# Layer 2's attention on one Trainium2 core: head scaling on GpSimd, other evictions, other waits

## The chip, the cores and the metric

The kernel runs on one core of one Trainium2 chip. The metric is the time of one launch on the device, in microseconds (us). Five runs of the kernel before gave 2965.73, 2966.24, 2966.6, 2967.86 and 2974.98; the median is 2966.6. A further execution was profiled and left the trace that is read here.

The engines are TensorE (PE in the profile; its weight loads are PEld), VectorE (DVE), ScalarE (ACT), GpSimd (POOL) and SyncE (SP, which issues most DMAs). SBUF is the on-chip memory with 128 partitions, PSUM the accumulators that TensorE writes. Each engine runs its own instructions in order and waits on semaphores for the others.

## The reference

The network has four layers of the form half feed-forward, attention, half feed-forward, on a residual of 2 batches x 1024 tokens x 128 features in f32. Layer 2 is the one that is changed:

```python
x = x + 0.5 * _L2_ffn_ref(_layernorm(x), ...)    # eight experts, top 2
x = x + _L2_attn_ref(_layernorm(x), ...)
x = x + 0.5 * _L2_ffn_ref(_layernorm(x), ...)
```

The attention has 16 heads of 64. Queries and keys are normalised per head, scores are clamped by a tanh, and the softmax runs over all 1024 keys:

```python
x = _rmsnorm(tokens, norm_w)
q, k, v = split(x @ Wq), split(k), split(v)        # k, v from x @ Wkv
q, k = _head_rmsnorm(q, q_gamma), _head_rmsnorm(k, k_gamma)
sim = jnp.tanh(einsum('bhid,bhjd->bhij', q, k) / 50) * 50 * 64 ** -0.5
out = einsum('bhij,bhjd->bhid', softmax(sim), v)
return out.reshape(b, n, 1024) @ Wo
```

with `_head_rmsnorm(x, gamma) = x / max(norm(x), 1e-12) * (gamma + 1) * 8`. The feed-forward sends each token to its two best of eight experts (128 to 512 and back, gelu), adds the input, normalises per expert and mixes the two results by their gates.

## The kernel before

The residual `x` stays in SBUF as [128, 16, 128]: 16 tiles of 128 tokens, in four chunks q = 0 to 3 of 512. Chunks 0 and 1 are batch 0, chunks 2 and 3 batch 1.

**Order.** TensorE's order is the order in which the Python code issues matmuls; the other engines' orders are chosen by the framework's scheduler from dependencies and modelled times. Side work is put into TensorE's order by threads: `c.later(key, pieces)` queues a list of functions and numbers, `c.tick(us)` advances a modelled clock, and a number in the list holds the thread back by so many modelled us before its next function. `c.need(key)` runs what is left of a thread at once. These numbers place work; they are not measured times.

**The mixture pass of layer 2** works on two halves of two chunks each: (0,1) and (2,3) before the attention, (0,2) and (1,3) after it. `l2_ffn_prep` (line 1227) normalises a chunk (`norm_pieces`, line 183: statistics on VectorE, apply as xn partly on ScalarE at line 164, transposes on TensorE at line 172) and stores it to DRAM as `xd`. After routing, `L2Experts` (line 1346) works on groups of up to four tiles of gathered tokens. `gather` (lines 1373 to 1382) reads a group's rows from `xd` into a buffer `xg` with one indirect DMA per tile, issued by GpSimd. `fetch` (line 1395) loads the experts' weights through SP. `ahead` (line 1404) decides how many groups are gathered in advance. A group is transposed (line 1428), multiplied (hidden at lines 1440 and 1449, output at 1456), combined on VectorE (lines 1474 to 1487; the last reader of `xg` is line 1474), and stored to DRAM as `yd` (line 1488). `l2_back` (line 1510) returns a half: sixteen indirect DMAs on GpSimd read rows of `yd` into `yg` (line 1525), and two `add` steps (lines 1532 to 1542, VectorE), one for each chunk, form the inverse standard deviation and add to `x`. After each, `l2_attn_prep` normalises that chunk for the attention.

**The attention** (`L2Attention`, line 1557) runs eight groups: batch b and f = 0 to 3, four heads each. `project(b, f)` makes two lists of eight pieces, one per tile j of 128 tokens:

- `product(j)`: matmuls for v (line 1583) and for q and k together (line 1587), into two of the shared PSUM banks; VectorE copies them to `v` (line 1584) and `raw` (line 1594); GpSimd squares `raw` into `sq` (line 1596); VectorE sums it per head into `hsq` (line 1597). After the eighth, `inv_sqrt` (lines 115 to 120, a bit trick and three Newton steps on VectorE) makes `hrq`, the inverse norms of all eight tiles.
- `turn(j)`: VectorE scales `raw` in place by `hrq` (line 1605), TensorE transposes it (`ppt`, line 1609), and VectorE writes it with the gains to `tr` (line 1612).

`run` works a group through in 16 slots. A slot computes scores for two key tiles (line 1673, four matmuls of 512 columns), ScalarE applies tanh (line 1680, twice) and exp (line 1681), and `mix` of the slot before adds up the probabilities and multiplies them by v (`po`, line 1706). The sums for the first half of the keys are made on GpSimd (`acp`: lines 1693, 1695, 1696), those for the second half on VectorE (`acc`: lines 1698 to 1702). After four slots `divide` sums `acc` over partitions (line 1718), copies to `rn` on ScalarE (line 1720), inverts it (line 1721) and scales `po` into `aoT` (line 1722), the last two on VectorE. The products of the next group are in slots 0 to 7, its turns in slots 10 to 14. The output projection of the group before stands in slots 8 and 9 (`py`, line 1650) and is added to `x` by VectorE (line 1659). Three `pe` buffers hold probabilities; two pairs of PSUM banks hold scores.

The first group has nothing to hide behind: `first` (line 1621) issues its products between the last experts and its turns after them, and the attention's first scores wait for all eight turns. The second half's return, called with `step` 1 in `l2_back`, runs during groups 0 and 1; the norms for the second mixture pass run in group 4 (chunks of batch 0), at the end of group 7 and behind it.

Of the kernel before, what the change touches and what calls it, by code (L numbers as in the profile page):

```python
# [11 lines left out]
F32 = mybir.dt.float32  # L12
# [3 lines left out]
ALU = mybir.AluOpType  # L16
# [3 lines left out]
P = 128  # L20
NT = 16
TB = 8
# [1201 lines left out]
    return h  # L1224


def l2_ffn_prep(c, w, keep, h, a):
    nc = c.nc
    q, r = h["qs"][a], {}
    tiles = slice(4 * a, 4 * a + 4)  # L1230
    norm = norm_pieces(c, r, q, by=8)

    def begin():
        if "o" not in h:
            h["o"] = keep.tile([P, 2, TB, 8], F32, tag="ho", name="ho", bufs=2)
            h["g"] = keep.tile([P, 2, TB], F32, tag="hg", name="hg", bufs=2)

    def store():
        nc.sync.dma_start(out=h["xd"][512 * a : 512 * a + 512, :].rearrange("(j p) d -> p j d", p=P), in_=r["xn"])

    def chosen():
        h["ready"] += 1
        if h["ready"] == 2:
            c.later(("route", h["name"]), l2_route(c, w, keep, h) + h["then"])

    gates = gate_pieces(
        c, r, q, w["router"], 8, w["beta"],
        places=lambda: ([h["o"][:, k, tiles, :] for k in range(2)], [h["g"][:, k, tiles] for k in range(2)]),
    )
    return [begin] + norm[:3] + [store] + norm[3:] + gates[:1] + [chosen] + gates[1:]  # L1250
# [95 lines left out]
class L2Experts:  # L1346
# [28 lines left out]
    def gather(self):  # L1375

        n = self.gathered
        h, g = self.groups[n]
        self.xg[n] = self.keep.tile([P, 4, P], F32, tag="xg", name="xg", bufs=4)
        for j, i in enumerate(g):  # L1380
            at = bass.IndirectOffsetOnAxis(ap=h["tok"][:, i : i + 1], axis=0)
            self.nc.gpsimd.indirect_dma_start(self.xg[n][:, j, :], None, h["xd"], at)
        self.gathered += 1
# [20 lines left out]
    def ahead(self, k):  # L1404

        h = self.groups[self.tiles[k][0]][0]
        if "tok" not in h:
            for a in range(2):
                self.c.need(("half", h["qs"][a]))
            self.c.need(("route", h["name"]))  # L1410

        some = 2 if any(self.c.waits(("back", h["name"])) for h in self.halves) else 3
        while self.gathered < min(self.tiles[k][0] + some, len(self.groups)) and self.routed(self.gathered):
            self.gather()
        while self.fetched < min(k + 6, len(self.tiles)) and self.routed(self.tiles[self.fetched][0]):
            self.fetch()
# [93 lines left out]
def l2_back(c, keep, h, parts, step):  # L1510


    nc = c.nc
    pieces = [[], []]
    for p, (a, j, done) in enumerate(parts):
        tiles = [(u, v) for u in range(2)[a] for v in range(4)[j]]
        b = {}

        def fetch(k, lo, tiles=tiles, b=b):
            if k + lo == 0:  # L1520
                b["yg"] = keep.tile([P, 2, 4, P + 1], F32, tag="yg", name="yg", bufs=2)
            for n in range(lo, lo + step):
                u, v = tiles[n]
                at = bass.IndirectOffsetOnAxis(ap=h["si"][:, TB * k + 4 * u + v :][:, 0:1], axis=0)
                nc.gpsimd.indirect_dma_start(b["yg"][:, k, n, :], None, h["yd"], at)

        def add(a=a, j=j, tiles=tiles, b=b, done=done):
            sc = keep.tile([P, 2, 4], F32, tag="bsc", name="bsc", bufs=2)
            var = keep.tile([P, 2, 4], F32, tag="bvar", name="bvar", bufs=2)
            yg = b["yg"]  # L1530

            c.tc.keep_in_program_order(nc.vector.tensor_copy(var, yg[:, :, :, P]))
            flat = lambda t: t.rearrange("p k n -> p (k n)")
            inv_sqrt(c, flat(sc), flat(var), 1.0 / P, 1e-6)
            g = h["g"].rearrange("p k (u v) -> p k u v", u=2)[:, :, a, j]
            nc.vector.tensor_tensor(
                sc.rearrange("p k (u v) -> p k u v", u=g.shape[2]), sc.rearrange("p k (u v) -> p k u v", u=g.shape[2]), g, ALU.mult
            )
            for n, (u, v) in enumerate(tiles):
                x = c.x[:, 4 * h["qs"][u] + v, :]  # L1540
                for k in range(2):
                    nc.vector.scalar_tensor_tensor(x, yg[:, k, n, 0:P], sc[:, k, n : n + 1], x, ALU.mult, ALU.add)
            done()

        gathers = [x for k in range(2) for lo in range(0, 4, step) for x in (partial(fetch, k, lo), 1.05 * step)]
        pieces[p] = gathers, add
    (one, add_one), (two, add_two) = pieces
    if step == 1:
        return [8.0] + one + two + [add_one, 14.0, add_two, 0.1]
    return [5.0] + one + two[:1] + [3.0, add_one, 1.2] + two[2:] + [8.0, add_two, 0.1]  # L1550


def l2_attn_prep(c, w, rs, q):

    e = float(np.finfo(np.float32).eps)
    return norm_pieces(c, rs[q], q, 1.0 + e, 1e-5 * e, w["norm"])


class L2Attention:
# [6 lines left out]
    def project(self, b, f):  # L1566


        c, nc, w, rs = self.c, self.c.nc, self.w, self.rs
        side, bank = self.side, c.bank  # L1570
        mine = self.pool if f % 2 else side
        raw = side.tile([P, TB, 2, 4, 64], F32, tag="raw", name="raw")
        tr = mine.tile([P, 2, 2, S], F32, tag="tr", name="tr", bufs=1)
        v = mine.tile([P, TB, 4, 64], F32, tag="v", name="v", bufs=1)
        ssq = side.tile([P, TB, 2, 4], F32, tag="hsq", name="hsq", bufs=2)
        rq = side.tile([P, TB, 2, 4], F32, tag="hrq", name="hrq", bufs=2)

        def product(j):
            c.need((self.key, 2 * b + j // 4))
            lhsT = rs[2 * b + j // 4]["xT"][:, j % 4 * P : (j % 4 + 1) * P]  # L1580
            pv = bank("pv")[:, 0:256]
            off = 1024 + f * 256
            nc.tensor.matmul(pv, lhsT=lhsT, rhs=w["wkv"][:, off : off + 256], start=True, stop=True)
            nc.vector.tensor_copy(v[:, j].rearrange("p h d -> p (h d)"), pv)
            pp = bank("pqk").rearrange("p (n h d) -> p n h d", n=2, h=4)
            for n, wt in enumerate((w["wq"], w["wkv"])):
                nc.tensor.matmul(
                    pp[:, n].rearrange("p h d -> p (h d)"),
                    lhsT=lhsT,
                    rhs=wt[:, f * 256 : (f + 1) * 256],  # L1590
                    start=True,
                    stop=True,
                )
            nc.vector.tensor_copy(raw[:, j], pp)  # L1594
            sq = side.tile([P, 2, 4, 64], F32, tag="sq", name="sq", bufs=1)
            nc.gpsimd.tensor_mul(sq, raw[:, j], raw[:, j])  # L1596
            nc.vector.tensor_reduce(ssq[:, j], sq, AX.X, ALU.add)
            if j == TB - 1:

                nc.vector.tensor_scalar(ssq, ssq, 1e-24, None, ALU.max)  # L1600
                inv_sqrt(c, rq, ssq, 1.0, 0.0)

        def turn(j):
            rj = raw[:, j]
            nc.vector.tensor_tensor(rj, rj, rq[:, j].unsqueeze(3).to_broadcast([P, 2, 4, 64]), ALU.mult)
            pt = bank("ppt").rearrange("p (n k t) -> p n k t", n=2, k=2)
            for n in range(2):
                for k in range(2):
                    nc.tensor.transpose(
                        pt[:, n, k, :], rj[:, n, 2 * k : 2 * k + 2, :].rearrange("p h d -> p (h d)"), c.ident  # L1610
                    )
            nc.vector.tensor_tensor(
                tr[:, :, :, j * P : (j + 1) * P],
                pt,
                w["gm"][:, :, 2 * f : 2 * f + 2].unsqueeze(3).to_broadcast([P, 2, 2, P]),
                ALU.mult,
            )

        return (tr, v), [partial(product, j) for j in range(TB)], [partial(turn, j) for j in range(TB)]
# [407 lines left out]
def macaron(ctx: ExitStack, tc: tile.TileContext, dram: dict, out: bass.AP):  # L2027
    nc = tc.nc
    c = Ctx(tc, dram)
# [34 lines left out]
    with ExitStack() as s1:  # L2064
        with tc.tile_pool(name="w0", bufs=1) as p0:
            w = l0_weights(c, p0)
            sets = l2_sets(c, dpool)
            r = [chunks() for _ in range(8)]
# [19 lines left out]
        w2 = l2_consts(c, keep2)  # L2088
        s2 = ctx.enter_context(ExitStack())
        wa = l2_attn_weights(c, s2.enter_context(c.pool("w2a")))  # L2090
        def halves(n, parts):

            hs = [l2_half(c, dpool, f"{n}{k}", qs) for k, qs in enumerate(parts)]

            def prep(q):
                h = next(h for h in hs if q in h["qs"])
                c.later(("half", q), l2_ffn_prep(c, w2, keep2, h, h["qs"].index(q)))

            return hs, prep

# [148 lines left out]
```

## Time and profile before

| | us |
|---|---|
| median of five runs | 2966.6 |
| profiled execution | 2975.98 |
| its span, first to last instruction | 2974.2 |
| first mixture pass of layer 2, experts | about 1616 to 1764 |
| attention, from its first scores | 1795.4 to about 2545 |
| second mixture pass | about 2550 to 2690 |

| group of the attention | 0 | 1 | 2 | 3 | 4 | 5 | 6 | 7 |
|---|---|---|---|---|---|---|---|---|
| first scores at, us | 1795.4 | 1883.2 | 1988.6 | 2076.6 | 2164.7 | 2272.8 | 2360.8 | 2448.8 |
| until the next group (7: its scores), us | 87.8 | 105.4 | 88.0 | 88.0 | 108.1 | 88.0 | 88.0 | 74.6 |

The granted clock of TensorE over the whole span is 0.94 of full speed. A line of the profile's groups names the line in the code, the engine, the operation, output and inputs, and how often it ran; then busy time and mean duration in ns, and the idle time ahead of it with what ended it. In the tables of stretches, each engine's busy us is followed by its number of instructions, then the granted clock, the share of DMA time and GB/s. In a timeline, start and duration stand first.

### The profile page before, as it was taken

The numbers are of one execution on the slowest core, as the hardware profiler recorded it, in microseconds if no ns is written. First come the engines' busy times: TensorE is split into PE (matmuls) and PEld (weight loads), VectorE is DVE, ScalarE is ACT, GpSimd is POOL, SyncE is SP. The second block draws the span as 40 slices with busy tenths as digits, with TensorE's granted clock in tenths as the row PEclk, the third lists the DMA queues.
The fourth block names the chain that finished last, engine by engine and source line by source line (L and its number), as shares of the span: only waits on it lengthen the run. The fifth ranks groups of instructions, "written<-read, shape, count | busy, mean of one in ns | idle before, by whom it ended". The sixth has DMA issues, their size and how long they took to land. (4 is left out here: it accounts for less than half of the span.)

```text
span 2974.2 us, 42437 instructions
## 1 busy us (share of the span) xinstructions
PE 2648.7 (89%) x14226; PEld 1511.3 (51%) x14226; DVE 2081.1 (70%) x6492; ACT 1605.3 (54%) x3188; POOL 953.1 (32%) x909
## 2 busy tenths in 40 slices
PE   7899999999989888888887959899998999879999
PEld 5544444444465455444445843334433433777667
DVE  4567667766646878868766567777777775668874
ACT  3355555555533355666632526667666778444553
POOL 0022122112102544445443445334543443342110
PEclk9899999999989868999997989999999999889999
DMA  5000000000000000000012730000000001660000
GB/s 124 8 15 15 15 8 15 15 15 8 8 22 1 1 1 1 1 1 2 18 40 73 207 84 9 1 1 1 1 1 8 1 28 39 164 176 22 1 5 11
DMA packets 69768, 86.52 MB, mean 29 GB/s; under 512 B 14334, under 2 KB 49935, under 8 KB 68912
## 3 DMA queue, kind: packets, MB, share of 16 engines
q1 hardware_dynamic: 56620, 70.14, 8.3%
q0 software_dynamic: 4992, 10.27, 1.7%
q10 hardware_dynamic: 7940, 3.41, 0.4%
q8 instruction: 114, 1.87, 0.2%
q14 instruction: 102, 0.84, 0.1%
HBM read 66.18 MB, written 12.38 MB: 26 GB/s over the span
## 5 line engine op out<-in xcount | busy, mean ns | idle before, releaser
L1680 ACT ACTIVATE pe<-ps 128x1024 f32<-128x1024 f32 x256 | 249.5, 1023 | 208.5 <-PE ps L1673 208.2
L507 ACT ACTIVATE pe<-ps,nm 128x512 f32<-128x512 f32 (+3 forms) x384 | 220.0, 579 | 113.8 <-DVE nm L505 111.9
L1673 PE MATMUL ps<-tr 64*128 64x512 f32 x1024 | 264.9, 637 | 0.0
L1706 PE MATMUL po<-pe,v 128*64 128x512 f32 x1024 | 250.8, 611 | 0.9 <-ACT pe L1681 0.9
L1681 ACT ACTIVATE pe<-pe 128x2048 f32<-128x2048 f32 x128 | 244.8, 1912 | 4.0
L341 DVE SCALAR_TENSOR_TENSOR x<-py,gates,x 128x128 f32<-128x128 f32 x448 | 134.0, 345 | 147.2 <-PE py L311 147.0
L494 PE MATMUL ps<-kT,qT 64*128 64x512 f32 (+3 forms) x768 | 181.7, 552 | 39.2 <-ACT pe L507 28.1
L505 DVE TENSOR_REDUCE nm<-ps 128x2 f32<-128x256 f32 (+1 forms) x192 | 182.9, 952 | 45.6 <-PE ps L494 42.8
L522 PEld LDWEIGHTS ptp<-ident,pe 128*128 128x128 f32 x1152 | 126.8, 143 | 113.8 <-issue 82.4
L522 PE MATMUL ptp<-ident,pe 128*128 128x128 f32 x1152 | 174.2, 287 | 4.7 <-ACT pT L104 2.2
L104 ACT COPY pT<-ptp 128x512 f32<-128x512 f32 x192 | 92.1, 480 | 159.8 <-PE ptp L522 158.4
L457 POOL TENSOR_TENSOR kT<-tab 128x512 f32<-128x512 f32 x32 | 54.4, 1699 | 367.1 <-DVE tab L456 367.0
L536 PE MATMUL po<-pT,v 128*64 128x512 f32 (+3 forms) x768 | 168.6, 518 | 0.0
L1449 ACT ACTIVATE hT<-ph,w1b 128x128 f32<-128x128 f32 x368 | 105.6, 369 | 100.7 <-issue 61.0
L1706 PEld LDWEIGHTS po<-pe,v 128*64 128x64 f32 x1024 | 62.8, 137 | 174.5 <-issue 159.7
L1693 POOL TENSOR_TENSOR acp<-pe 128x1024 f32<-128x1024 f32 x32 | 78.3, 2446 | 220.5 <-ACT pe L1681 197.3
L1673 PEld LDWEIGHTS ps<-tr 64*128 64x128 f32 x1024 | 91.2, 192 | 104.7 <-issue 73.0
L1058 POOL TENSOR_SCALAR pe<-pe,rs 128x256 f32<-128x256 f32 (+7 forms) x128 | 95.2, 756 | 138.7 <-DVE rs L1055 55.9
L311 PEld LDWEIGHTS py<-l3f_w,hT 128*128 128x128 f32 x1024 | 125.6, 196 | 24.5 <-issue 20.3
L1596 POOL TENSOR_TENSOR sq<-raw 128x512 f32<-128x512 f32 x64 | 88.7, 1385 | 141.2 <-DVE raw L1594 107.0
L1440 PE MATMUL ph<-xgT,w1b 128*128 128x128 f32 x736 | 111.0, 299 | 22.6 <-ACT hT L1449 12.6
L494 PEld LDWEIGHTS ps<-kT,qT 64*128 64x128 f32 x768 | 60.7, 192 | 136.9 <-ACT pe L507 62.9
(418 smaller groups left out, 6340.4 us busy)
## 6 DMA issues: line engine op xcount, KB each, us to landing
w1b<-sets SPq DMA_DIRECT2D x92, 258.0 KB, 5.0
b2g<-sets SPq DMA_DIRECT2D x92, 128.0 KB, 4.3
two<-two SPq DMA_DIRECT2D x64, 128.0 KB, 2.3
yd<-y SPq DMA_DIRECT2D x20, 258.0 KB, 4.7
l2f_w<-in_l2f_w SPq DMA_DIRECT2D x2, 2048.0 KB
sets<-in_l2f_w SPq DMA_DIRECT2D x1, 2048.0 KB
xd<-xn SPq DMA_DIRECT2D x8, 256.0 KB, 3.6
l3f_w<-in_l3f_w SPq DMA_DIRECT2D x2, 1024.0 KB
```

Of the source, the lines that this page charges most:

```text
L311: nc.tensor.matmul(py[:, j, :], lhsT=hT[:, k, j * P : (j + 1) * P], rhs=w2[:, e, k, :], start=(k == 0), stop=(k == hc - 1),)
L341: c.nc.vector.scalar_tensor_tensor(x, py[:, j, :], rs[q]["g"][:, j, e : e + 1], x, ALU.mult, ALU.add)
L494: nc.tensor.matmul(ps[:, h, :W], lhsT=u["qT"][r, q0 : q0 + P], rhs=u["kT"][r, gk * 512 : gk * 512 + W], start=True, stop=True,)
L505: nc.vector.tensor_reduce(nm, ps[:, :, :W], AX.X, ALU.max, negate=True)
L507: nc.scalar.activation(u["pe", n][:, h, i, :W], ps[:, h, :W], AF.Exp, bias=nm[:, h : h + 1], accum_out=u["rs"][:, n, i, h : h + 1],)
L522: nc.tensor.transpose(pt[:, i * P : (i + 1) * P], u["pe", n][:, h, i, j * P : (j + 1) * P], c.ident)
L536: nc.tensor.matmul(u["po", n][r, lo * P :], lhsT=u["v"][:, BLOCKS[n][1] * 4 + j, cols], rhs=u["pT", n, j][h][:, lo * P :], start=(j == 0), ...
L1440: nc.tensor.matmul(ph[:, a * P : (a + 1) * P], lhsT=t[:, a * P : (a + 1) * P], rhs=xT[n][:, j * P : (j + 1) * P], start=True, stop=True,)
L1673: nc.tensor.matmul(ps[:, h, :], lhsT=tr[r, 1, p, k * P : (k + 1) * P], rhs=tr[r, 0, p, q * 512 : (q + 1) * 512], start=True, stop=True,)
L1680: nc.scalar.activation(pe[:, j], ps, AF.Tanh, scale=1.0 / 50.0)
L1681: nc.scalar.activation(pe, pe, AF.Exp, scale=50.0 * 0.125)
L1706: nc.tensor.matmul(u["po"][r, :], lhsT=u["v"][:, k, 2 * u["p"] + h, :], rhs=pe[:, j, h, :], start=(k == 0), stop=(k == TB - 1),)
```

## The change

Five edits, all in layer 2:

1. Head scaling: `raw` times `hrq` moves out of `turn`'s own place into `scale(j)`. Turn 0 issues the scales of tiles 0, 1 and 2, turn j that of tile j + 2. It runs on GpSimd, except in the first group, where even tiles stay on VectorE. There are 64 such instructions in all, eight in a group.
2. In the first group, the PSUM copies to `v` and `raw` run on ScalarE instead of VectorE.
3. `xg` has six buffers instead of four, and groups are gathered up to five ahead instead of two or three.
4. The return of the second half (`step` 1) waits 40 modelled us instead of 8.
5. The waits ahead of a norm's apply and of its transposes become (10, 9) instead of (4.5, 4) for two kinds of chunk: chunks 2 and 3 in the attention's norm, and chunks 0 and 1 in the second mixture pass. All other chunks of these two functions keep (4.5, 4).

```diff
-def l2_ffn_prep(c, w, keep, h, a):
+def l2_ffn_prep(c, w, keep, h, a, late):
...
-    norm = norm_pieces(c, r, q, by=8)
+    norm = norm_pieces(c, r, q, by=8, wait=(4.5, 4.0) if late else (10.0, 9.0))
...
-        self.xg[n] = self.keep.tile([P, 4, P], F32, tag="xg", name="xg", bufs=4)
+        self.xg[n] = self.keep.tile([P, 4, P], F32, tag="xg", name="xg", bufs=6)
...
-        some = 2 if any(self.c.waits(("back", h["name"])) for h in self.halves) else 3
-        while self.gathered < min(self.tiles[k][0] + some, len(self.groups)) and self.routed(self.gathered):
+        while self.gathered < min(self.tiles[k][0] + 5, len(self.groups)) and self.routed(self.gathered):
             self.gather()
...
     if step == 1:
-        return [8.0] + one + two + [add_one, 14.0, add_two, 0.1]
+        return [40.0] + one + two + [add_one, 14.0, add_two, 0.1]
...
-    return norm_pieces(c, rs[q], q, 1.0 + e, 1e-5 * e, w["norm"])
+    return norm_pieces(c, rs[q], q, 1.0 + e, 1e-5 * e, w["norm"], wait=(4.5, 4.0) if q < 2 else (10.0, 9.0))
...
-        mine = self.pool if f % 2 else side
+        mine, first = self.pool if f % 2 else side, b == f == 0
...
-            nc.vector.tensor_copy(v[:, j].rearrange("p h d -> p (h d)"), pv)
+            copy = nc.scalar.copy if first else nc.vector.tensor_copy
+            copy(v[:, j].rearrange("p h d -> p (h d)"), pv)
...
-            nc.vector.tensor_copy(raw[:, j], pp)
+            copy(raw[:, j], pp)
...
+        def scale(j):
+            rj = raw[:, j]
+            e = nc.vector if first and j % 2 == 0 else nc.gpsimd
+            e.tensor_tensor(rj, rj, rq[:, j].unsqueeze(3).to_broadcast([P, 2, 4, 64]), ALU.mult)
+
         def turn(j):
+
+            for k in (0, 1, 2) if j == 0 else (j + 2,):
+                if k < TB:
+                    scale(k)
             rj = raw[:, j]
-            nc.vector.tensor_tensor(rj, rj, rq[:, j].unsqueeze(3).to_broadcast([P, 2, 4, 64]), ALU.mult)
...
-                c.later(("half", q), l2_ffn_prep(c, w2, keep2, h, h["qs"].index(q)))
+                c.later(("half", q), l2_ffn_prep(c, w2, keep2, h, h["qs"].index(q), n == 1 or q >= 2))
```

In the changed kernel's numbering the lines of this part stand 1 or 2 lower up to the projection (gathered rows are transposed at 1426, `v` is copied at 1583, `raw` at 1593) and 7 higher after it: scale 1605, `ppt` 1616, `tr` 1619, output projection 1657, its add to `x` 1666, scores 1680, tanh 1687, exp 1688, `acp` 1700 to 1703.

The engines' orders follow from the scheduler. Of the built program: TensorE's order differs from before only in the places of the transposes at line 172 for chunks 2 and 3 (group 1, slots 12 and 15 instead of 5 and 8) and of the norm and router steps in groups 4 and 5, two slots later. On GpSimd, all gathers of `xg` stand ahead of the sixteen of `yg` in the first mixture pass; at its end come seven squares, two gathers of `yg`, a square, seven gathers, four scales, seven gathers. In each later group the order is the eighth square, scale 0, the acp of slot 8's first key tiles, scales 1 to 7, and that sum's two further acp. On SP, the loads of layer 3's weights wait for the attention's last `aoT`, since the allocator places them elsewhere; before, they ran in its last group.

## The prediction

> **What bounds the kernel now.** I read the page's shares first, then TensorE's waits by line, then busy time stretch by stretch, then the order of work on the engines that feed TensorE.
>
> ```profile
> PE 2648.7 (89%) x14226; PEld 1511.3 (51%) x14226; DVE 2081.1 (70%) x6492; ACT 1605.3 (54%) x3188; POOL 953.1 (32%) x909
> ```
>
> TensorE bounds nearly everything, so only its gaps and its clock can give time. In layer 2 the waits (line, releaser: total us, times, longest) and the stretches (length, busy per engine, granted clock) are:
>
> ```profile
> PE pt L172 <- ACT xn L164: 17.1, 4, 8.2
> PE ppt L1609 <- DVE raw L1605: 13.2, 4, 10.3
> PE pt L1428 <- DMA xg<-xd,r_tok: 11.6, 4, 5.0
> PE py L1650 <- DVE x L1659: 5.1, 5, 1.0
> PE ppt L1609 <- DVE x L1659: 4.8, 4, 1.2
> PE pt L1428 <- DVE v L1584: 4.7, 1, 4.7
> ...
> 1700.00:1750.00 50.00, 33.90 (x234) 29.89 (x232) 29.10 (x137) 16.89 (x55) 24.71 (x25) 0.86 0.55 142
> 1750.00:1800.00 50.00, 32.72 (x155) 24.21 (x156) 33.79 (x113) 7.83 (x21) 21.10 (x21) 0.73 0.14 39
> 1883.00:1989.00 106.00, 92.76 (x396) 38.46 (x396) 79.78 (x168) 67.53 (x59) 38.15 (x20) 0.94 0.00 1
> 1989.00:2077.00 88.00, 85.01 (x386) 35.34 (x384) 67.20 (x78) 63.44 (x53) 40.86 (x20) 1.00 0.00 1
> ```
>
> The first two stretches are the end of the first mixture pass and the first head group's projection: TensorE is idle a third of the time, at a clock of 0.86 and 0.73. Groups 2, 3, 5 and 6 (such as 1989:2077) take 88.0 us with 85.0 busy. Groups 1 and 4 take 105.4 and 108.1: residual adds, norms and routing of token chunks run in them, and line 172 waits for ScalarE's xn.
>
> What matters for a move from VectorE to GpSimd is how they meet:
>
> ```profile
> 2039.01 2.25 DVE L119 SCALAR_TENSOR_TENSOR nw<-nh,nw 128x64 f32<-128x64 f32 x1
> 2044.93 7.68 DVE L1605 TENSOR_TENSOR raw<-raw,hrq 128x512 f32<-128x512 f32 x6
> ...
> 2038.77 2.41 POOL L1693 TENSOR_TENSOR acp<-pe 128x1024 f32<-128x1024 f32 x1 [1.47 <-ACT pe L1681]
> 2044.54 2.35 POOL L1695 TENSOR_TENSOR acp<-acp,pe 128x1024 f32<-128x1024 f32 x1 [3.36 <-ACT pe L1681]
> 2046.97 2.69 POOL L1696 TENSOR_TENSOR acp<-acp,pe 128x1024 f32<-128x1024 f32 x1
> ...
> L719 POOL TENSOR_TENSOR eq<-eq,fi 128x512 f32<-128x512 f32 x32 | 33.8, 1056 | 34.0 <-DVE fi L718 20.3 <-DVE ln_rs L120 9.7 <-DVE md L129 3.0
> ```
>
> A 0.23 us VectorE operation took 2.25 because GpSimd's acp ran; six scales of 0.68 took 7.68 instead of 4.1 beside two acp; the second acp grew from 2.35 to 2.69. Instructions with two SBUF operands wait for the other engine's whole instruction, and they alternate. Copies from PSUM, reductions and reciprocals were not slowed.
>
> **The change, part by part.** All figures are against the profiled execution: 2975.98 us, span 2974.2, so 1.8 outside it, which is left alone. It is 9.4 above the median of 2966.6; savings are subtracted from the median.
>
> *End of the first mixture pass (six xg buffers, eager gathers).* Sixteen yg gathers (1699.0 to 1719.3, 1.25 us each) stand on GpSimd ahead of the last seven xg gathers. TensorE then waits 4.96, 1.91 and 2.99 us (1717.9 to 1729.2) and 1.07 for xn. In the changed order all xg gathers precede the yg ones; the last waits only for the buffer released before 1689.5. The three waits go, but line 172 needs the norm whose scale VectorE finishes at 1722.67; 0.88 for two xn on ScalarE gives 1723.6. It started at 1730.8: gain 7.
>
> *First group's evictions on ScalarE.* VectorE's queue delays the 4.66 us wait at 1746.8 (on v's copy, behind a residual add and norm) and waits of 1.03, 0.41 and 1.35 among the last products. ScalarE is idle for most of 1736 to 1770 and a 128x512 copy from PSUM costs it 0.57 to 0.59: the 4.66 falls to about 0.6, gain 4. Its cover is that idle ScalarE; without it, eight tiles x (0.58 + 0.4) = 8 us. Four products are left after the experts. They began at 1764.8, and the last square ended at 1781.2, as copies, squares and five yg gathers followed one another; at 1.75 us a product on TensorE (0.43 each for its matmul pairs, plus a copy), they take 1764.8 + 7 + 0.6 + 1 + 1 = 1774.4 (the last copy, its square, and what two gathers hold that up): gain 6.7. Together the last square ends 17.7 earlier, near 1763.5.
>
> *The scales of that group.* Even tiles stay on VectorE, odd ones go to GpSimd, where seven of the second half's yg gathers stand ahead: 7 x 1.25 = 8.8, to 1772.3. That the 40 us wait sends this return into the attention is not what the issue order shows. Four scales at 1.04 to 1.3 end at 1777 and the last turn, with its tr, at 1779. Attention began at 1795.4: 16.4, less 1.4 because TensorE still idles before the turns and starts them, as now (1778.7 to 1799.2), at half clock: **15 gained**. Ends: 8 (only the gathers and copies, scales at 1.70 as line 457 has on average) and 18 (no gathers ahead).
>
> *Group 0* has 6.5 us more than a steady group in its slots 8 to 13, where the first half-return's add lies. It moves to group 1: **4.5**, between 0 and 6.5.
>
> *Steady groups.* Each has a 1.02 and a 1.20 wait for x (line 1659), queued behind the eight scales. These go: 2.2. GpSimd gets eight operations of about 1.05 (line 719: same shape, same broadcast factor), in a burst of seven before the two acp of k2=1. These end up to 1.1 later, and tr(1) of slot 11 waits behind the acc that needs them: 0.5 given back. 1.7 x 4 = **6.8**; between 4 x 2.2 = 8.8 and, with scales of 1.7 to 1.9, 4 x -2 = -8.
>
> *Group 1.* Both adds and both norms now come after hrq, at about 2041 in the coordinates of the group shown. There GpSimd has scale, acp, seven scales, two acp: 8 x 1.05 + 3 x 2.35 = 15.5. VectorE's chain (nine steps of inverse root, eight adds, statistics, nine steps again, ln_off) is some 30 tiny instructions with two SBUF operands, 0.16 to 0.27 each; its first ten each wait for one whole GpSimd instruction. Its end, 2052 without that (2041 plus 5 for the add, as at 1931.3 to 1936.2, and 6 for the norm), becomes about 2066; two xn of 0.88 stand on ScalarE between the tanh of slot 10, and that slot's second tanh, due at 2049, runs at 2068, with the exp and the next scores behind it: TensorE stops about 18 us. The second norm costs 5, half clock after both 3.5 each (as after the gaps of 1919 and 1944, for 7 us each): 85.8 + 18 + 5 + 7 = 115.8 against 105.4: **10.4 lost**. Ends: a stop of 5 and 4 at the clock (95.4, 10 gained), and 14 lost (scales at 1.5: 8 x 0.45).
>
> *Group 4.* The xn of the next pass's norm moves ahead of the exp of slot 9. ScalarE waits there about 12.8 us, of which TensorE has 9 of stop, then 4 for the second norm, 4 at half clock, 6 of transposes and routing: 85.8 + 23 = 108.8 against 108.1: **0.9 lost** (−8 to +9, by the same arithmetic).
>
> *The second mixture pass.* A shift in the allocator's addresses makes layer 3's weights (two loads of 1 MB and fourteen small ones) wait for the last aoT instead of hiding in the last group. They stand on SP's queue ahead of the eighth tile set and the last xd store (issued 2553 and 2554), delaying both by 4 to 6 us; the first is needed near 2567, so **1 lost**, between 0 and 8.
>
> Sum: 15 + 4.5 + 6.8 − 10.4 − 0.9 − 1 = 14.0.
>
> The Trainium skill, "Perfetto Trace Analysis", Optimizing Scalar/DVE Operations, warns that these two engines share an SBUF read port, so that moving work between them might not help; taken literally, the steady groups' term would be 0 and the sum 7. The rows favour a part of the gain, since what goes are two waits, not work. "GPSIMD Engine Reference", Engine selection, puts two-input elementwise work at about twice VectorE's time; as an estimate from the row of 0.68 that is 1.36 per scale, 0.3 over line 719, and the sum would be 14.0 − 7 x 0.3 x 2 = 9.8.
>
> **The rivals.**
> *A, little collision.* If VectorE's tiny steps slip between GpSimd's instructions, group 1 gains 10, group 4 breaks even and the steady groups get their 8.8: 15 + 4.5 + 8.8 + 10 − 1 = 37, so 2929. For it: the six scales lost 3.6 us to two acp of 5.0 together, less than one for one. Against it: the 0.23 us step that cost 2.25.
> *B, slower.* The chain in group 1 against GpSimd's burst, with ScalarE blocked at xn behind it. Price: group 1 −14, group 4 −8 by the same stop, steady groups −8 as each scale is stretched; gains shrink to 8 + 2; second pass −1: −21, so 2988. It decides from the point where the chain ends over 30 us after hrq (the forecast has 25).
> *C, nothing.* The first pass's gain halves, because the odd scales wait for all 14 yg gathers left (17.5 us instead of 8.8), and steady groups gain 0.5 each: 6 + 4.5 + 2 − 10.4 − 0.9 − 1 = 0, so 2966. For it: gathers of 1.25 us ran without a pause from 1781.4 to 1795.5. Against it: the issue order has half of them behind the scales.
> That the half-return isn't delayed past the odd scales (the change not doing what it says) is in the forecast with 8.8.
>
> **How the numbers follow.** The forecast holds .38, A .25, B .23, C .14. 2966.6 − 14.0 = 2952.6. Its own range is 2942 to 2964; with A (2929, and 3 + 2 + half of group 4's 9 beyond it, from the upper ends above) and most of B the range is 2920 to 2985. About 0.2% (6 us) is what this kernel's runs can tell from no change: faster holds A and the forecast less a little (.62), within it C and a bit of the forecast (.15), slower B (.23).
>
> **What would show it.** xg waits at line 1426 gone and line 172 near 1723; attention starting near 1779; steady groups at 86 us, without the waits of lines 1657 and 1616 on x; scale on GpSimd at 1.04 to 1.3; a TensorE gap of 15 to 20 us in group 1, released by xn. The prediction is wrong if that gap is under 8 (A), if the scales take over 1.6, or if attention starts after 1787.

## The result, and the profile after

| | before | after |
|---|---|---|
| median, us | 2968.1 (44 runs) | 2968.91 (24 runs) |
| ratio after to before | | 1.0001 (0.9995 to 1.0007) |
| profiled execution's span, us | 2974.2 | 2961.7 |

The change makes no difference: 14 us faster were forecast. A second comparison on the same kind of chip gave 0.9997 (0.9988 to 1.0005). The two profiled spans differ by 12.5 us, which misleads: single executions of either kernel differ by several us in layers that the change does not touch (the experts of layer 2 began between 1614 and 1625 us in the profiles of this study, with no order among the kernels). So stages are compared inside layer 2, with a second profile of each kernel on such a chip beside the first. Stage lengths in us, first profile / second:

| | before | after | forecast of the difference | found |
|---|---|---|---|---|
| first gathered tile to last expert output | 144.0 / 144.0 | 138.5 / 138.8 | | −5.3 |
| last expert output to first scores | 30.7 / 30.0 | 27.8 / 27.8 | −15 for both | −2.5 |
| group 0 | 87.8 / 85.4 | 86.1 / 86.1 | −4.5 | −0.5 |
| group 1 | 105.4 / 105.2 | 113.1 / 113.0 | +10.4 | +7.7 |
| groups 2, 3, 6, each | 88.0 | 86.1 | −1.7 | −1.9 |
| group 4 | 108.1 | 109.6 / 109.5 | +0.9 | +1.5 |
| group 5 | 88.0 | 89.4 | −1.7 | +1.4 |
| last scores to the second pass's first gathered tile | 23.1 | 21.2 / 21.3 | | −1.8 |
| second pass, to its last output | 132.9 / 133.1 | 132.2 / 132.3 | +1 for both | −0.7 |

With group 7's 0.8 the found column sums to −5: less than half of the forecast, and still more than the medians show (between 3.6 us faster and 1.5 slower in the second comparison).

The waits of TensorE in layer 2, in the profile after:

```profile
PE ph L1438 <- ACT hT L1447: 12.4, 23, 1.6
PE po L1713 <- ACT pe L1688: 11.4, 3, 7.4
PE ppt L1616 <- DVE raw L1605: 9.6, 1, 9.6
PE pt L172 <- DVE tr L1619: 8.8, 3, 5.7
...
PE ps L1680 <- ACT pe L1687: 8.1, 1, 8.1
...
PE pt L172 <- ACT xn L164: 6.8, 2, 5.1
PE ph L1438 <- ACT xn L164: 6.2, 1, 6.2
...
PE py L1657 <- DVE x L1666: 5.2, 1, 5.2
...
PE pt L1426 <- DMA xg<-xd,r_tok: 3.2, 3, 1.6
```

The waits for `v` (but for 0.2 us) and the 1.0 and 1.2 us waits for x are gone. So are the three waits for xg ahead of line 172; the 3.2 us that are left lie at the start of the pass. In their place stand waits for xn, for `tr` and for `pe`, whose writer ScalarE was itself held up by xn, and one long wait for x.

Busy time by stretch: the end of the first mixture pass, group 1 and group 2.

```profile
1700.00:1750.00 50.00, 37.17 (x258) 35.30 (x257) 30.56 (x155) 22.41 (x70) 17.68 (x19) 0.88 0.49 140
1750.00:1800.00 50.00, 34.51 (x169) 22.49 (x170) 26.46 (x71) 19.34 (x27) 32.58 (x29) 0.81 0.11 31
1870.00:1983.00 113.00, 93.35 (x393) 39.34 (x392) 86.23 (x160) 66.44 (x58) 48.21 (x28) 0.89 0.00 1
1983.00:2069.00 86.00, 84.92 (x387) 35.40 (x385) 56.81 (x70) 63.15 (x54) 48.93 (x28) 1.00 0.00 1
```

Group 2 does the same TensorE work in 86 us, with VectorE at 56.8 instead of 67.2. In group 1 VectorE has no scales any more and is yet busier, 86.2 instead of 79.8: its instructions are stretched. TensorE's clock there fell from 0.94 to 0.89. The timeline of group 1, VectorE first, then GpSimd, then ScalarE:

```profile
1922.96 0.90 DVE L115 TENSOR_SCALAR nh<-bvar 128x8 f32<-128x8 f32 x1
1923.89 2.29 DVE L116 TENSOR_SCALAR bsc<-nh 128x8 int32<-128x8 int32 x1
1926.21 0.96 DVE L118 TENSOR_TENSOR nw<-bsc 128x8 f32<-128x8 f32 x1
1927.21 0.97 DVE L119 SCALAR_TENSOR_TENSOR nw<-nh,nw 128x8 f32<-128x8 f32 x1
1928.21 0.97 DVE L120 SCALAR_TENSOR_TENSOR bsc<-nw,bsc 128x8 f32<-128x8 f32 x1
...
1922.75 1.07 POOL L1605 TENSOR_TENSOR raw<-raw,hrq 128x512 f32<-128x512 f32 x1 [3.89 <-DVE hrq L120]
1923.79 2.36 POOL L1700 TENSOR_TENSOR acp<-pe 128x1024 f32<-128x1024 f32 x1
1926.11 7.04 POOL L1605 TENSOR_TENSOR raw<-raw,hrq 128x512 f32<-128x512 f32 x7
...
1936.45 1.02 ACT L1687 ACTIVATE pe<-ps 128x1024 f32<-128x1024 f32 x1 [10.03 <-PE ps L1680]
1947.03 0.88 ACT L164 ACTIVATE xn<-x,ln_off,ln_rs 128x128 f32<-128x128 f32 x2 [9.55 <-DVE ln_off L152]
1947.81 1.00 ACT L1687 ACTIVATE pe<-ps 128x1024 f32<-128x1024 f32 x1
```

Steps that take 0.17 us alone take 0.97: one per scale. The second tanh of slot 10 waits behind xn until 1947.8, 25 us after hrq.

### The profile page after: what moved, and what is told of

Same layout as the page of the kernel before. It is cut to its first block, busy times and chain, and to the rows that moved or that the text cites. A ratio compares the mean times of both kernels' runs of the same rounds, so it can differ in the third digit from the quotient of the medians.

```text
span 2961.7 us, 42481 instructions
## 1 busy us (share of the span) xinstructions
PE 2634.4 (89%) x14226; PEld 1505.9 (51%) x14226; DVE 2019.6 (68%) x6416; ACT 1606.7 (54%) x3204; POOL 1014.0 (34%) x969
## 5 line engine op out<-in xcount | busy, mean ns | idle before, releaser
L1700 POOL TENSOR_TENSOR acp<-pe 128x1024 f32<-128x1024 f32 x32 | 76.4, 2388 | 174.1 <-ACT pe L1688 174.0
L1728 DVE RECIPROCAL rn<-rn 128x512 f32<-128x512 f32 x32 | 107.1, 3346 | 35.9 <-ACT rn L1727 35.9
```

## The experiments

The kernels ran on chips of two kinds. On one kind (call it A) the kernel before takes 2965 to 2970 us, on the other (B, two chips) 3054, mostly because both mixture passes are longer there. Ratios are to the kernel before on the same chip.

**Two profiles more of the kernel before**, one on each kind, with no edit.

> The kernel before, unchanged, for a second profile. Theory 1 (each stage's length belongs to the kernel, and what differs between two executions lies elsewhere): attention groups again 87.8, 105.4, 88.0, 88.0, 108.1, 88.0, 88.0 us within 0.5, and 162 to 164 us from the experts' first weights transposed to the first scores as in the first profile; the span differs from 2974 by up to 8 us, in other layers. Rival (the first profile of the kernel before had a slow layer 2): the attention or the first mixture pass is 5 us or more shorter than in the first profile.

> The kernel before once more, for a profile that says what its first one owed to that execution. Where the experts' weights arrive in time: theory 3 (the first profile's layer 2 was ordinary, and the 8 us by which that execution stood above the median lay in layers 0, 1 and 3): first gathered tile to first scores 174 to 176 us again, attention 729.5. Rival (the gathers and weights of the first mixture pass were late in that execution): 166 to 170 us, and the changed kernel's gain there was an accident.

On B (3056.64 us): groups 89.1, 105.1, 88.0, 88.0, 108.1, 88.0, 88.0, as in the first profile but for 1.3 in group 0; first pass 177.6 instead of 144.0, second 169.9 instead of 132.9. On A (2968.78 us): 174.0 us from the first gathered tile to the first scores, attention 726.7 because group 0 took 85.4. So the attention's stages belong to the kernel, the first profile was ordinary in the first pass, and the rival falls.

**The changed kernel again**, on B and on A.

> The changed kernel, unchanged, for a second profile and a second ratio. Theory 1: attention groups again 86.1, 113.1, 86.1, 86.1, 109.6, 89.4, 86.1 us within 0.5 and a ratio of 0.9995 to 1.0007 that these stages do not explain by themselves. Rival: the stages of layer 2 come out 5 us or more longer than in the first profile, which explains the equal medians.

> The changed kernel once more, beside the best version on one chip. Theory 3: first gathered tile to first scores 164 to 168, attention 733 us, ratio 0.998 to 1.001, the gain of the first mixture pass being larger than the 3.8 us lost in the attention by 3 to 5 us at most. Rival: 170 or more to the first scores, ratio 1.000 or more.

On A: 0.9997, 166.6 us to the first scores, attention 733.3. On B it is slower: 1.0069 (1.0056 to 1.0082). The attention is the same there; the first pass takes 183.9 against 177.6 and the second 184.1 against 169.9. The first pass of the kernel before on A (its second profile), both passes of it on B, and both of the changed kernel on B:

```profile
1617.00:1761.00 144.00, 116.19 (x884) 107.25 (x883) 83.89 (x396) 63.12 (x205) 59.95 (x63) 0.91 0.60 160
```

```profile
1623.00:1801.00 178.00, 120.48 (x887) 112.60 (x887) 84.34 (x396) 62.79 (x205) 59.53 (x63) 0.86 0.49 130
2580.00:2750.00 170.00, 114.54 (x861) 109.00 (x860) 81.75 (x416) 66.13 (x213) 54.27 (x61) 0.84 0.51 131
```

```profile
1619.00:1803.00 184.00, 122.79 (x884) 116.17 (x884) 80.23 (x388) 66.72 (x213) 59.38 (x63) 0.82 0.46 125
2584.00:2768.00 184.00, 116.30 (x867) 111.09 (x866) 83.19 (x430) 67.27 (x215) 53.32 (x63) 0.83 0.50 134
```

The work is the same, and every engine's share is smaller on B, that of the DMA engines too (0.60 on A, 0.49 and 0.46 on B): something delays the experts' work there, and the change makes it worse. What it is was not found. Other profiles on B show how far single ones scatter: with edit 1, 2, 4 or 5 alone (the runs below) the first pass took 176 to 181 us and the second 173 to 176, and with all edits but the scaling 184 and 187. So a part of both differences is scatter, and what is left as the cause is edit 3, the buffers and gathers, which was not run alone on B.

**The scaling alone**, and the change without it.

```diff
-            nc.vector.tensor_tensor(rj, rj, rq[:, j].unsqueeze(3).to_broadcast([P, 2, 4, 64]), ALU.mult)
+            for k in (0, 1, 2) if j == 0 else (j + 2,):
+                if k < TB:
+                    scale(k)
```

> The kernel before with the head scaling on GpSimd two tiles ahead, nothing else. Theory 1 (the scale itself pays where VectorE has no long chain, and costs where a chain of small steps follows hrq): groups 2, 3, 5, 6 at 86.1, group 1 within 3 of 105, because its first norm comes before hrq; the first scores 4 to 8 us later than before, as the odd scales stand behind the gathers of yg; ratio 0.998 to 1.001. Rival (GpSimd's burst hurts everywhere): steady groups at 88 or more, ratio over 1.002.

> The kernel before with the head scaling on GpSimd alone, where the experts' weights arrive in time. Theory (the parts add up to nothing: scaling, evictions and gathers gain what return and norms lose): attention 719 to 720 us as on the other chip, last output to first scores 33 instead of 30; ratio 0.997 to 0.999. Rival (the first half of the change was worth little and the second half harmless): 0.9995 or more.

> The changed kernel with the head scaling back on VectorE inside each turn, all else as changed. Theory 1 (what is lost in group 1 is the alternation of VectorE's chain with GpSimd's burst of scales): group 1 falls from 113.1 to about 101, steady groups return to 88.0, first scores 2 to 6 us earlier; ratio to the kernel before 0.993 to 0.997. Rival (the loss is the place of the adds and norms, not the scales): group 1 stays at 110 or more, ratio 1.000 or more.

The scaling alone, both times on B (the second expectation was for A): 0.9983 (0.9973 to 0.9992) and 0.9981 (0.9972 to 0.9990); steady groups 86.1, group 1 105.3 and 105.6, attention 720 and 721 against 729.5; 33 us from the last expert output to the first scores instead of 30, so 3 later where 4 to 8 were expected. The move itself pays 5 to 6 us. The change without it (on B): 1.0071 (1.0058 to 1.0084), group 1 at 107.1, so without the burst it is 6 us shorter than the changed kernel's 113.0 but still 2 over before. Steady groups are back at 88.0, and group 0 takes 92.0. My expected 101 was wrong: the late adds and norms cost something without the burst too.

**The return and the norms taken back**, one, the other, or both (all on A).

```diff
-        return [40.0] + one + two + [add_one, 14.0, add_two, 0.1]
+        return [8.0] + one + two + [add_one, 14.0, add_two, 0.1]
```

> The changed kernel with only the return's wait back at 8; the norms' waits stay (10, 9). Theory 2: the first add goes back to group 0 and the second to the early slots of group 1, so group 1 is 103 to 108 instead of 113.1; group 0 at most 2 longer; groups 4 and 5 stay at 109.6 and 89.4. Rival (the late norms alone cost group 1): group 1 stays over 111.

```diff
-    norm = norm_pieces(c, r, q, by=8, wait=(4.5, 4.0) if late else (10.0, 9.0))
+    norm = norm_pieces(c, r, q, by=8, wait=(4.5, 4.0))
...
-    return norm_pieces(c, rs[q], q, 1.0 + e, 1e-5 * e, w["norm"], wait=(4.5, 4.0) if q < 2 else (10.0, 9.0))
+    return norm_pieces(c, rs[q], q, 1.0 + e, 1e-5 * e, w["norm"], wait=(4.5, 4.0))
```

> The changed kernel with only the norms' waits back at (4.5, 4); the return's wait stays 40. Theory 2: groups 4 and 5 return to 107.5 and 86.2, 5 us together; group 1 stays at 110 or more, because both adds follow hrq and meet the burst of scales. Rival (the late norms alone cost group 1): group 1 falls to 106.

> The changed kernel with the return's wait back at 8 and the norms' waits back at (4.5, 4): scaling on GpSimd, evictions on ScalarE and six xg buffers remain. Theory 2 (the return and the norms cost what the other edits gain): attention groups as with the scaling alone, 86, 105, 86, 86, 107.5, 86, 86, 75, together 718 us against 732 for the changed kernel; ratio 0.0045 below the changed kernel's on the same sort of chip, 0.9955 where the expert weights arrive in time and about 1.0025 where the second mixture pass waits for them. Rival (the adds of the return disturb wherever they stand): group 0 or 1 grows by what group 1 loses, together 728 or more.

| | ratio | group 1 | groups 4 + 5 | attention |
|---|---|---|---|---|
| changed kernel | 0.9997 (0.9988 to 1.0005) | 113.0 | 198.9 | 733.3 |
| return at 8 | 0.9952 (0.9938 to 0.9967) | 101.7 | 197.5 | 720.0 |
| norms at (4.5, 4) | 0.9976 (0.9966 to 0.9986) | 113.6 | 193.6 | 726.7 |
| both | 0.9961 (0.9947 to 0.9976) | 105.4 | 193.5 | 719.3 |

The wait of 40 costs 0.45%, some 13 us, of which 11 are in group 1. Group 1 with the return at 8:

```profile
1878.00:1979.50 101.50, 90.98 (x394) 37.37 (x392) 74.64 (x160) 66.56 (x59) 48.02 (x28) 0.95 0.00 1
```

VectorE is busy 74.6 us instead of 86.2 with the same number of instructions (160), and TensorE's clock is 0.95: the adds run before hrq, where GpSimd has only a square or an acp now and then. The later norms cost 4 to 5 us in groups 4 and 5, and gain 4 in group 1 once the return is early.

**The late return and the late norms, each alone in the kernel before** (both on B; the edits are the changed kernel's own lines for them).

> The kernel before with only the return's wait at 40. Theory (both adds behind hrq delay what waits for VectorE in group 1, with or without GpSimd's burst): group 0 loses 1 to 2.5, group 1 grows by 4 to 10; ratio 1.001 to 1.003. Rival (only the burst of scales makes the late return harmful): group 1 within 1 of 105, ratio 1.000.

> The kernel before with only the norms' waits at (10, 9) for the attention's chunks 2 and 3 and the second mixture pass's chunks 0 and 1. Theory: group 1 falls to about 102, as in the version with the return at 8, groups 4 and 5 grow by 1 to 5 together; ratio 0.9985 to 1.001. Rival (late norms cost in both places): group 1 over 106, ratio over 1.002.

The return at 40: 1.0015 (1.0003 to 1.0027), group 1 at 107.2, which is 2 longer and not 4 to 10. The norms: 1.0027 (1.0017 to 1.0037), group 1 at 108.5 where 102 was expected, groups 4 and 5 together 198.1 instead of 196.1. So the late return needs the burst to be dear: with the burst it costs 8 to 11 us in group 1, without it 2, or nothing where the norms are late too (107.1 in the changed kernel without the scaling, 108.5 with the norms alone). And the late norm helps group 1 only where the scales have left VectorE. Without that, line 172's second transposes (chunk 3) wait 4.9 us for x, and x stands behind six scales, which take 8.0 us beside two acp, and a reciprocal of 3.3. In the kernel with the return alone the longest wait is again for xn:

```profile
PE pt L172 <- ACT xn L164: 13.4, 1, 13.4
```

**The evictions alone** (on B).

```diff
+            copy = nc.scalar.copy if first else nc.vector.tensor_copy
+            copy(v[:, j].rearrange("p h d -> p (h d)"), pv)
```

> The kernel before with the first group's evictions on ScalarE alone. Theory (the wait for v behind VectorE's add turns into one for xn at the head of ScalarE's queue): first gathered tile to last output within 1.5 of 144, last output to first scores 27 to 28 instead of 30; ratio 0.998 to 1.000. Rival (as the prediction had it, 4 gained before the last output and 7 behind it): ratio 0.996.

0.9997 (0.9987 to 1.0006). From last output to first scores it is 25.3 instead of 30.4, so that part works; but group 0 takes 92.2 instead of 89.1, since its first slot takes 5.2 us instead of 3.4 and its second 10.4 (9.0 in the kernel before on that kind of chip, 6.3 with the scales on GpSimd). Before the last output 1 us is gained (176.5 against 177.6), which is within the scatter, and a wait of TensorE that the kernel before did not have appears:

```profile
PE ph L1440 <- ACT xn L164: 6.2, 1, 6.2
```

**The gathers alone** (on A).

```diff
-        self.xg[n] = self.keep.tile([P, 4, P], F32, tag="xg", name="xg", bufs=4)
+        self.xg[n] = self.keep.tile([P, 4, P], F32, tag="xg", name="xg", bufs=6)
...
-        while self.gathered < min(self.tiles[k][0] + some, len(self.groups)) and self.routed(self.gathered):
+        while self.gathered < min(self.tiles[k][0] + 5, len(self.groups)) and self.routed(self.gathered):
```

> The kernel before with six xg buffers and gathers five ahead, nothing else. Theory: the waits for xg before the last two groups go, line 172 starts about 7 us after the last output instead of 14, and the first scores come 4 to 8 us earlier; layer 3's weights move behind the attention; groups as before (729.5 together); ratio 0.997 to 0.999 where weights arrive in time. Rival (the norm of chunk 0 holds it up instead): no gain to the first scores, ratio 1.000.

0.9991 (0.9982 to 1.0001): not told apart from nothing. In the profile the first pass is 4.9 us shorter, and line 172 has the wait that remains, for xn, as the prediction had it:

```profile
1728.70 1.11 PE L172 MATMUL pt<-ident,xn 128*128 128x128 f32 x4 [5.38 <-ACT xn L164]
```

**Fewer buffers, and the best version.** The first is the version with return and norms both taken back, with five xg buffers instead of six. In the best one, also with five, the attention's norms of chunks 2 and 3 stay at (10, 9). The last run is the best one with six.

```diff
-        self.xg[n] = self.keep.tile([P, 4, P], F32, tag="xg", name="xg", bufs=6)
+        self.xg[n] = self.keep.tile([P, 4, P], F32, tag="xg", name="xg", bufs=5)
```

> As the kernel with three edits, but with five xg buffers, so that layer 3's weights are loaded in the attention's last group again as before and only the last gathered group stands among the gathers of the return. Theory 2: the stretch from the last scores to the end of the second mixture pass is no longer than in the kernel before, where six buffers cost it up to 15 us on the chip of the first runs; ratio 0.994 to 0.997 on either sort of chip. Rival (the gathers ahead, not layer 3's weights, hold up the experts' weights): no difference from six buffers.

> Scaling on GpSimd, evictions on ScalarE, five xg buffers, the return's wait at 8, the norms of the second mixture pass at (4.5, 4) and only the attention's norms of chunks 2 and 3 at (10, 9). Theory 2: group 1 at 101.7 as with the return at 8, groups 4 and 5 at 107.5 and 86.2, attention 716 us instead of 733; layer 3's weights loaded in the last group; ratio 0.994 to 0.9955. Rival (the stages do not add up): 0.996 or more, as with three edits.

> The best version once more. On a chip where the kernel before takes 2965 to 2970: ratio 0.994 to 0.997 again. On one where it takes 3054: attention 717 us as before, second mixture pass 170 to 176 us from the first gathered tile to the last output, as in the kernel before, since layer 3's weights are loaded earlier; ratio 0.994 to 0.997 there too. Rival (on such a chip any change of the gathers costs): second mixture pass 182 or more, ratio 1.000 or more.

> The best version with six xg buffers, so that layer 3's weights are loaded behind the attention as in the changed kernel. On a chip where the kernel before takes 2965 to 2970: no difference from five buffers by more than 0.1%. On one where it takes 3054: second mixture pass 184 us as in the changed kernel, ratio 0.003 to 0.005 above the one with five buffers. Rival: the same as five buffers on either sort of chip, so that the longer second pass comes from the gathers five ahead.

All met chips of kind A. Five buffers: 0.9964 (0.9951 to 0.9978), as with six. Best: 0.9955 (0.9942 to 0.9968) and 0.9948 (0.9932 to 0.9963); with six buffers 0.9939 (0.9925 to 0.9952). Attention 716.5, 715.6 and 716.4 us; group 1 at 102.2, 101.6 and 101.7. This beats both kernels by about 0.5%. The place of layer 3's weights makes no difference on A that can be seen. In the changed kernel SP issues the first of them behind the attention (2447.5 before):

```profile
2535.39 0.34 SPq L54 DMA_DIRECT2D l3f_ln1w<-in_l3f_ln1w  x1
```

Whether this is what lengthens the second pass on B was not tried there: no run with five buffers met such a chip. The longer first pass can't come from it, since these loads come some 780 us later.

## Why the prediction was wrong

The time lies inside the range, but the likeliest case was a gain of 14, and rival C's result came. C had the first pass's gain halved, and it was, but by another cause than C gave; and C's steady groups were wrong. The step that failed most is the end of the first mixture pass: moving the first group's copies to ScalarE was to turn a wait of 4.66 us into 0.6, and the wait came back as one of 6.2 us for xn. Next come group 0, whose 4.5 were not there to be had, and group 5. Of the 9 us between the forecast's 14 and the stages' 5 these are 7.2, 4.0 and 3.1; group 1, the second pass and the other steady groups came out better than forecast. The other 5, between stages and medians, stay open.

- **End of the first mixture pass: mis-sized, 15 forecast and 7.8 found.** The gathers behaved as worked out: with both profiles set to the start of their first gathered tile, line 172 began 6.0 us earlier, for 7. What failed is "the 4.66 falls to about 0.6, gain 4". I read that wait as one for a copy in VectorE's queue. Moving the copy left what stood ahead of it, the second chunk's add and norm, and its xn now stands in ScalarE's queue ahead of the next gelu. In the changed kernel (VectorE, ScalarE, TensorE):

```profile
1731.16 0.69 DVE L1596 TENSOR_REDUCE hsq<-sq 128x8 f32<-128x512 f32 x1 [8.84 <-POOL sq L1595]
1731.77 0.16 DVE L1530 COPY bvar<-yg 128x8 f32<-128x8 f32 x1
...
1744.69 0.88 ACT L164 ACTIVATE xn<-x,ln_off,ln_rs 128x128 f32<-128x128 f32 x2 [4.56 <-DVE ln_off L152]
...
1746.01 2.05 PE L1438 MATMUL ph<-xgT,w1b 128*128 128x128 f32 x8 [6.21 <-ACT xn L164]
```

VectorE sits idle for 8.8 us because the first hsq stands ahead of the add; the chain ends in xn at 1744.7, and TensorE waits 6.2 us where it waited 4.7. The same wait in the kernel with the evictions alone shows that it belongs to them. Mostly by it, the last square ended at 1767.9, where the forecast, moved by the 2.9 us by which this execution began earlier, had 1760.6. The seven gathers ahead of the odd scales were right: 1768.1 to 1776.6, then four scales in 4.04.
- **Group 0: wrong.** Its excess was set down to the add. With the add gone it takes 86.1, and in the second profile of the kernel before it took 85.4 with the add in it. Its slots 8 to 13, where the excess was seen, took 34.7 and 33.9 us in the two profiles before and 34.0 with the add gone and the scaling still on VectorE: there was next to nothing to gain. In the changed kernel they took 34.7 again, because the burst brings a wait of its own. VectorE's acc waits for GpSimd's acp, which stands behind seven scales; `tr` follows it, and TensorE waits 4.1 us for `tr`:

```profile
1850.63 1.23 DVE L1707 TENSOR_TENSOR acc<-acc,acp 128x1024 f32<-128x1024 f32 x1 [7.67 <-POOL acp L1703]
1851.77 0.69 DVE L1619 TENSOR_TENSOR tr<-ppt,l2gm 128x512 f32<-128x512 f32 x1
...
1852.60 1.09 PE L1616 MATMUL ppt<-ident,raw 128*128 128x128 f32 x4 [4.08 <-DVE tr L1619]
```

The prediction had such a term, 0.5 us, for the steady groups and none for this one.
- **Steady groups: right.** 1.9 each, scales at 1.04 us. The Trainium skill's doubt ("Perfetto Trace Analysis", Optimizing Scalar/DVE Operations), that moving work between these two engines might not help, does not hold in these groups, and does in group 1 (105.3 and 105.6 with the scaling alone, 105.1 before). "GPSIMD Engine Reference", Engine selection, has about twice VectorE's time for such an operation; here it is 1.04 against 0.68 for a scale, though 2.35 against 1.22 for a sum of 128x1024.
- **Group 1: right in mechanism, near in size.** 7.7 lost for 10.4. The alternation one for one and the chain ending 25 us after hrq came as worked out. The single gap of 15 to 20 us did not appear, for the stop is split: 5.2 us for x, which stands in VectorE's queue amid the chain and which the forecast overlooked, 8.1 for scores behind the tanh, 5.7 for tr behind the second chain. The runs add that the return's wait is the cause: with 8 in place of 40 the group takes 101.7.
- **Group 4: right** (+1.5 for +0.9; the prediction's own terms, 108.8 against 108.1, make 0.7). **Group 5: overlooked.** Two of its first slots took 7.0 and 7.7 us instead of 5.3 and 6.6, since the router's last steps of the second pass moved into them. That is 3.1 us more than "1.7 gained".
- **Second mixture pass: wrong sign, small.** 2.5 us were gained, most of it ahead of the first gathered tile. That the earlier gathers did it is not shown: on B this stretch takes 21 us in kernels with the old gathers too. The late weights did not show on A.
- **What stays open.** The stages add up to 5 us faster, the medians to nothing. The same gap of 1 to 10 us stands between stages and ratio in every kernel on A with five or six buffers, the gathers alone among them (8 by the stages, 2.7 by the ratio), while those kernels differ from one another about as their stages do: the return's wait is worth 13 us by both. So part of the first pass's gain that the profiles show may not be there in an ordinary execution. Single profiles may also just scatter that much: layer 2 took 3.4 us less in the second profile of the kernel before than in the first, and on B the gap goes the other way (the scaling alone gains 0 to 2 us by its two profiles against the one of the kernel before, 5 to 6 by the ratio). This was not settled.

Part by part, then (the scaling and evictions measured on B, the rest on A): the scaling gains 5 to 6 us, gathers and evictions some 3 and 1, which can't be told from nothing, and the late return and late norms together take 0.36% away again, 11 us.

## What to carry to other kernels

Before moving an instruction off a busy queue, ask what stands ahead of it there, and whether the queue that it goes to holds a wait for the same thing: a wait for a copy was really one for a norm, and came back as a longer one. In this kernel the burst on GpSimd cost little beside VectorE's long instructions (the steady groups gained 1.9 us each) and much beside a chain of tiny ones: place such chains before the burst, and ask what else stands behind the burst on GpSimd (an acp, in group 0). Where a change bundles several edits, take each away once: here two of five cancelled the rest. Without them the kernel is 0.4% faster than before, and 0.5% with only the attention's norms kept late.

## What was not expected of the hardware

VectorE instructions with one SBUF operand were held up too: lines 115 and 116 (a tensor and constants) took 0.90 and 2.29 us beside GpSimd, 0.17 alone, though the prediction named only those with two. "SBUF — State Buffer", Who interferes with whom, says that `tensor_scalar` can take the pair of ports that VectorE shares with GpSimd; the rows agree. GpSimd lost nothing by it in this stretch: seven scales took 7.04 us, 1.0 each, no more than their median of 1.04, while each VectorE step took as long as a scale. It is not always so: in the kernel with the return at 8, a square beside VectorE's acc and adds took 1.96 us, where one alone takes 1.04. And chips differ: the same program, kernel before, takes 2968 us on one kind and 3054 on another, 71 of the 86 us in the two passes that load weights by the tile, and a change that is neutral on the one costs 0.7% on the other.
